# Splitting a pair's TensorE transposes in a pre-norm block's query sweep, and copying the value operands from SBUF

## The chip, the cores and the metric

The kernel runs on one core of one Trainium2 chip. The metric is device microseconds from launch to end; before the change the median of three runs is 2529.96 us (2529.02 to 2530.29).

## The reference

One pre-norm transformer block on 2048 tokens of width 1024, in fp32. The attention goes over the 32 heads *within* each token (32 x 32 scores a token), and the feed-forward weights are rounded to 16 levels (NF4) and scaled back by each block's largest magnitude before use.

```python
def attn(h):                                   # h: 1 x 2048 x 1024
    q = (h @ wq.T + bq).reshape(B, S, H, D)    # H = D = 32
    k = (h @ wk.T + bk).reshape(B, S, H, D)
    v = (h @ wv.T + bv).reshape(B, S, H, D)
    scores = einsum('bshd,bstd->bsht', q, k) / sqrt(D)
    return einsum('bsht,bstd->bshd', softmax(scores), v).reshape(B, S, E)

def ffn(h):
    gate = einsum('bsd,hd->bsh', h, nf4(w1))   # w1, w2: 2752 x 1024
    up   = einsum('bsd,hd->bsh', h, nf4(w2))
    return einsum('bsh,dh->bsd', silu(gate) * up, nf4(w3))

x = x + attn(layernorm(x))
x = x + ffn(layernorm(x))
```

## The kernel before

There are four stages: a sweep for the queries, one for the keys, one for the values with the attention's output, and the feed-forward part. Each sweep goes over eight pairs of 128-token tiles. A pair's projection is a 2 x 2 block product done with seven block products instead of eight (Strassen's scheme in Winograd's form). `products()` does the seven in a fixed order: B11, T3, T2, B21, T1, B22, T4, named by the weight operand. The left operands are seven blocks of the tile `A`: the transposed input blocks `SA11`, `SA12`, `SA22` (and `SA21` in a tile of its own, `a21`), and `S1` to `S4`, the sums and differences that `differences()` forms on VectorE (lines 383 to 386). Each product is eight TensorE matmuls. Products that share a PSUM bank accumulate: bank `z` takes B11, T2, T1; bank `q` takes T3 and T4; in the queries' sweep B22 has its own bank `y`. ScalarE copies a stage of a bank out (line 345), and VectorE adds it to another (lines 362, 366, 374 and 377) to give the two output tiles `ce` and `co`. Line 377 is the last reader of bank `q`; the next pair's T3 writes that bank, which has one buffer.

Between products `products()` calls `fill(n)`, with n running 7, 6, 2, 5, 3, 4. There the sweep places other work in TensorE's order. In the queries' sweep, `fill(5)` (between T1 and B22) holds the next pair's sixteen 128 x 128 transposes (line 458): per tile j two groups of four, each into one PSUM tile `pt` out of three. ScalarE copies each `pt` twice: as it is to `A` (line 461), and with its columns in another order to `V` (line 462), from which the values' sweep's operands are formed by the same `differences()` and stored to DRAM (`opV`, line 473). `A` is stored too (`opD`, line 469), for the keys' sweep. `V` has one buffer: the next pair's copies into it wait until this pair's store of `V` has been read out.

Beside all this runs `background()`, a generator that rounds the feed-forward weights: for each chunk some fifteen VectorE passes over 128 x 1024 numbers (lines 221 to 230), most of them fed by a ScalarE pass into `sg` (line 229), with ScalarE scalings in sixteen pieces before and after (line 182). `advance(n)` emits n of its steps; `flush()` emits the TensorE transposes of a finished chunk (line 156), four at a time. The queries' sweep emits seven steps a pair.

The order of TensorE's instructions is that of the program text. On the other engines and the DMA queue of SyncE a planner orders the instructions at compile time, by the place in the program and by when it expects operands to be ready; on the chip each engine then takes its own list strictly in that order.

Of the kernel before, what the change touches and what calls it, by code (L numbers as in the profile page):

```python
# [14 lines left out]
ALU = mybir.AluOpType  # L15
# [53 lines left out]
def preln_block_kernel(  # L69
# [14 lines left out]
    nc = tc.nc  # L84
# [89 lines left out]
    def flush(steps=3):  # L174
        for _ in range(steps):
            if pending and next(pending[0], flush) is flush:
                pending.pop(0)
# [69 lines left out]
    def advance(n):  # L247
        for _ in range(n):
            next(bg, None)
# [23 lines left out]
    SA11, SA12, SA22, S1, S2, S3, S4 = range(7)  # L273
# [50 lines left out]
    def mm4(dst, w, xop, start, stop):  # L324
        for k in range(4):
# [7 lines left out]
            )  # L333

    def products(A, fill, used=lambda name: None, apart=None):

        def mul(dst, a, w, start, stop):
            mm4(dst, A[:, a], W[w], start, stop)  # L340
            used(w)

        def copied(nm, src):
            t = pair.tile([P, TB], FP, tag=nm, name=nm)
            nc.scalar.copy(t, src)  # L345
            return t

        z = ps_pj.tile([P, TB], FP, tag="z", name="z")
        mul(z, SA11, "B11", True, False)
        g0 = copied("g0", z)  # L350
        q = ps_pj.tile([P, TB], FP, tag="q", name="q")
        mul(q, S3, "T3", True, False)
        s7 = copied("s7", q)
        fill(7)
        mul(z, S2, "T2", False, False)
        u2 = copied("u2", z)
        fill(6)
        r = bank("r")
        mul(r, SA12, "B21", True, True)
        ce = pair.tile([P, E], FP, tag="C0", name="ce")  # L360
        co = pair.tile([P, E], FP, tag="C1", name="co")
        nc.vector.tensor_tensor(ce[:, 0:512], g0, r, ALU.add)
        fill(2)
        mul(z, S1, "T1", False, apart is not None)
        u4 = copied("u4", z)
        nc.vector.tensor_tensor(co[:, 512:], u4, s7, ALU.add)
        fill(5)
        if apart is None:
            mul(z, S4, "B22", False, True)
            nc.scalar.copy(ce[:, 512:], z)  # L370
        else:
            y = apart.tile([P, TB], FP, tag="y", name="y", bufs=1)
            mul(y, S4, "B22", True, True)
            nc.vector.tensor_tensor(ce[:, 512:], u4, y, ALU.add)
        fill(3)
        mul(q, SA22, "T4", False, True)
        nc.vector.tensor_tensor(co[:, 0:512], u2, q, ALU.add)
        fill(4)
        return ce, co

    def differences(t, a21):

        nc.vector.tensor_tensor(t[:, S1], a21, t[:, SA22], ALU.add)
        nc.vector.tensor_tensor(t[:, S2], t[:, S1], t[:, SA11], ALU.subtract)
        nc.vector.tensor_tensor(t[:, S3], t[:, SA11], a21, ALU.subtract)  # L385
        nc.vector.tensor_tensor(t[:, S4], t[:, SA12], t[:, S2], ALU.subtract)

    def qk_T(t, c, b):

        nc.vector.transpose(t, c.rearrange("p (h d) -> p h d", d=D))  # L390
        nc.vector.tensor_tensor(t, t, b.unsqueeze(2).to_broadcast([P, 32, 32]), ALU.add)
# [43 lines left out]
    def load_x(i):  # L435
        xt[i] = work.tile([P, E], FP, tag="x", name="xt", bufs=2)
        nc.sync.dma_start(xt[i], xf[ts(i, P), :])
# [4 lines left out]
    class Inputs:  # L442
# [9 lines left out]
            self.v21 = work.tile([P, 4, P], FP, tag="V21", name="V21")  # L452

        def transposes(self, j):
            for half in range(2):
                pt = ps_t.tile([P, 4, P], FP, tag="pt", name="pt")
                for k in range(4):
                    nc.tensor.transpose(pt[:, k, :], self.xn[j][:, ts(4 * half + k, P)], ident)
                n = (SA11, SA12, SA21, SA22)[2 * j + half]
                a, v = (self.a21, self.v21) if n == SA21 else (self.A[:, n], self.V[:, n])  # L460
                nc.scalar.copy(a, pt)
                nc.scalar.copy(
                    v.rearrange("p k (c m) -> p k c m", c=4),
                    pt.rearrange("p k (m c) -> p k c m", c=4),
                )

        def finished(self):
            differences(self.A, self.a21)
            nc.sync.dma_start(opD[self.p], self.A)

        def finished_v(self):
            differences(self.V, self.v21)
            nc.sync.dma_start(opV[self.p], self.V)
# [12 lines left out]
    nxt = Inputs(0)  # L486
# [9 lines left out]
    def weight_chunk(m, k):  # L496

        b = {}
        for nm in ("B11", "B12", "B21", "B22"):
            b[nm] = work.tile([P, TB], FP, tag=f"c{nm}", name=f"c{nm}")  # L500
            nc.sync.dma_start(b[nm], block(m, int(nm[1]) - 1, int(nm[2]) - 1)[:, k, :])
        t3 = work.tile([P, TB], FP, tag="cT3", name="cT3")
        nc.vector.tensor_tensor(t3, b["B22"], b["B12"], ALU.subtract)
        nc.vector.tensor_tensor(b["B12"], b["B12"], b["B11"], ALU.subtract)
        nc.vector.tensor_tensor(b["B22"], b["B22"], b["B12"], ALU.subtract)
        nc.vector.tensor_tensor(b["B21"], b["B21"], b["B22"], ALU.subtract)
        for n, t in ((1, b["B12"]), (2, b["B22"]), (3, t3), (4, b["B21"])):
            nc.sync.dma_start(wtD[m, n][:, k, :], t)

    def next_W(m):  # L510
        return lambda name: load_W(m, name)

    def load_A(src, p):
        t = pair.tile([P, 7, 4, P], FP, tag="A", name="A", bufs=2)
        nc.sync.dma_start(t, src[p])
        return t

    for p in range(NP):
        more = p + 1 < NP
        now = nxt  # L520
        if more:
            load_x(2 * p + 2)
            load_x(2 * p + 3)
            nxt = Inputs(p + 1)

        def fill(n):
            if n in (7, 3):
                flush(1)
            if n == 5 and more:
                nxt.transposes(0)  # L530
                nxt.transposes(1)
            advance(0 if n == 5 else 1)

        cs = products(now.A, fill, (lambda name: None) if more else next_W("k"), ps_t)
        flush(1)
        if more:
            nxt.finished()
        for j in range(2):
            t = work.tile([P, 32, NH], FP, tag="qd", name="qd", bufs=2)
            qk_T(t, cs[j], qb_sb)  # L540
            nc.sync.dma_start(qD[2 * p + j], t)
        now.finished_v()
        weight_chunk("kv"[p // 4], p % 4)
        advance(2)
        if p == NP - 2:
            first = load_A(opD, 0)
# [63 lines left out]
    for p in range(NP):  # L610
# [12 lines left out]
        for j in range(2):  # L623
            t = work.tile([P, 32, NH], FP, tag="kd", name="kd", bufs=3)
# [74 lines left out]
    for p in range(NP):  # L699
# [32 lines left out]
        for j in range(2):  # L732
            t = work.tile([P, 32, D], FP, tag="vd", name="vd", bufs=3)
# [325 lines left out]
```

## Time and profile before

| | us |
|---|---|
| median of the runs | 2529.96 |
| the profiled execution's own time | 2526.8 |
| span of that execution, first to last instruction | 2525.0 |
| TensorE busy (share of the span) | 2445.7 (97%) |
| VectorE busy | 1923.1 (76%) |
| ScalarE busy | 1564.9 (62%) |
| queries' sweep: start of the first product to start of the keys' first | 13.00 to 244.44 |

TensorE is busy 97% of the span, at a mean granted clock of 0.991. The queries' sweep is the first 10% of the span; in it VectorE is almost as busy as TensorE. A product takes 3.43 us from its start to that of the next one; four 128 x 128 transposes take 0.44 us.

In a timeline's line the first number is the start in us, the second the time the merged instructions took; the bracket at the end is the engine's idle time before them, and what ended it.

### The profile page before, as it was taken

The numbers are of one execution on the slowest core, as the hardware profiler recorded it, in microseconds if no ns is written. First come the engines' busy times: TensorE is split into PE (matmuls) and PEld (weight loads), VectorE is DVE, ScalarE is ACT, GpSimd is POOL, SyncE is SP. The second block draws the span as 40 slices with busy tenths as digits, with TensorE's granted clock in tenths as the row PEclk, the third lists the DMA queues.
The fourth block names the chain that finished last, engine by engine and source line by source line (L and its number), as shares of the span: only waits on it lengthen the run. The fifth ranks groups of instructions, "written<-read, shape, count | busy, mean of one in ns | idle before, by whom it ended". The sixth has DMA issues, their size and how long they took to land.

```text
span 2525.0 us, 36235 instructions
## 1 busy us (share of the span) xinstructions
PE 2445.7 (97%) x14160; PEld 1146.6 (45%) x14160; DVE 1923.1 (76%) x2088; ACT 1564.9 (62%) x3147; POOL 104.9 (4%) x152
## 2 busy tenths in 40 slices
PE   8999999999998999999999999999999999999998
PEld 4444455544444444444444444444444444444433
DVE  8999788878898578978789788887878878851022
ACT  3556544344543478878788787888877888851100
POOL 1010000000000000010000100001000010000100
PEclk9999999999999999999999999999999999999999
DMA  8779633656678574453743547436375353641574
GB/s 306 298 287 358 234 142 129 240 193 214 222 231 298 171 229 113 146 142 134 241 121 136 135 145 238 129 112 159 126 227 151 116 146 126 226 133 63 109 287 141
DMA packets 145323, 464.04 MB, mean 184 GB/s; under 512 B 12352, under 2 KB 66624, under 8 KB 125312
## 3 DMA queue, kind: packets, MB, share of 16 engines
q1 hardware_dynamic: 133056, 419.73, 45.9%
q0 software_dynamic: 11520, 41.95, 9.9%
q8 instruction: 111, 1.82, 0.3%
q14 instruction: 60, 0.49, 0.1%
q10 hardware_dynamic: 576, 0.05, 0.0%
HBM read 275.82 MB, written 185.86 MB: 183 GB/s over the span
## 4 chain that ended last, share of the span: by engine, by line
DVE 29%; PE 25%; ACT 11%; issue 4%; DMA 1%; DVEq 0%; ACTq 0%
DVE r L230 21%; PE po L951 12%; PE z L326 7%; ACT wn L182 4%; ACT r L182 3%; PE q L326 3%; ACT sg L229 2%; DVE r L223 2%; DVE r L225 2%; PE rr L326 1%; DVE am L194 1%; DVE r L241 1%; ACT wop L157 1%; PE po L963 1%; PE ptw L156 0%
## 5 line engine op out<-in xcount | busy, mean ns | idle before, releaser
L229 ACT ACTIVATE sg<-wn 128x1024 f32<-128x1024 f32 x780 | 814.3, 1051 | 358.1 <-DVE r L230 351.5
L230 DVE SCALAR_TENSOR_TENSOR r<-sg,r 128x1024 f32<-128x1024 f32 x780 | 946.9, 1214 | 68.5 <-ACT sg L229 26.2
L951 PE MATMUL po<-w,h 128*128 128x512 f32 x1344 | 594.0, 596 | 6.6 <-ACT acc L975 3.2
L951 PEld LDWEIGHTS po<-w,h 128*128 128x128 f32 x1344 | 250.0, 190 | 324.2 <-issue 288.3
L326 PE MATMUL z<-xB,w 128*128 128x512 f32 x720 | 325.4, 600 | 3.5 <-ACT u L889 1.8
L326 PE MATMUL z<-xT,w 128*128 128x512 f32 x656 | 296.3, 594 | 5.2 <-ACT u L882 5.0
L326 PE MATMUL q<-xT,w 128*128 128x512 f32 x656 | 290.9, 592 | 0.0
L182 ACT ACTIVATE wn<-wn,rc 128x64 f32<-128x64 f32 x1032 | 262.2, 336 | 45.1 <-DVE rc L202 45.1
L326 PEld LDWEIGHTS z<-xB,w 128*128 128x128 f32 x720 | 134.6, 192 | 166.9 <-issue 151.7
L326 PEld LDWEIGHTS q<-xT,w 128*128 128x128 f32 x656 | 123.6, 190 | 151.4 <-issue 149.2
L326 PEld LDWEIGHTS z<-xT,w 128*128 128x128 f32 x656 | 121.9, 190 | 153.9 <-issue 138.2
L326 PE MATMUL q<-wT,A 128*128 128x512 f32 x384 | 174.5, 598 | 2.3 <-DVE A L385 2.3
L326 PE MATMUL z<-wT,A 128*128 128x512 f32 x384 | 175.5, 600 | 1.1 <-ACT u L345 0.8
L326 PE MATMUL z<-wB,A 128*128 128x512 f32 x320 | 152.0, 619 | 13.4 <-ACT u L345 13.4
L182 ACT ACTIVATE r<-r,am 128x64 f32<-128x64 f32 x608 | 153.8, 339 | 14.7 <-DVE r L230 14.7
L326 PE MATMUL rr<-xB,w 128*128 128x512 f32 x328 | 147.5, 592 | 0.0
L975 ACT COPY acc<-po 128x512 f32<-128x512 f32 x160 | 91.3, 571 | 73.0 <-PE po L951 71.3
L194 DVE TENSOR_REDUCE am<-wn 128x16 f32<-128x1024 f32 (+1 forms) x65 | 78.4, 1206 | 76.1 <-ACT r L182 70.0
L981 POOL DMA_DIRECT2D x1d<-acc x80 | 70.2, 877 | 1497.3 <-ACT acc L975 1497.3
L326 PEld LDWEIGHTS q<-wT,A 128*128 128x128 f32 x384 | 72.6, 192 | 90.4 <-issue 84.8
L326 PEld LDWEIGHTS z<-wT,A 128*128 128x128 f32 x384 | 70.3, 190 | 79.8 <-issue 76.7
L885 DVE TENSOR_TENSOR g<-g,rr 128x512 f32<-128x512 f32 x41 | 28.0, 682 | 102.4 <-PE rr L326 102.4
(112 smaller groups left out, 2100.5 us busy)
## 6 DMA issues: line engine op xcount, KB each, us to landing
w<-wd SPq DMA_DIRECT2D x41, 1280.0 KB, 6.9
wd<-wop SPq DMA_DIRECT2D x21, 2048.0 KB, 6.7
x1d<-acc POOLq DMA_DIRECT2D x80, 512.0 KB, 5.1
wn<-in_w_dram SPq DMA_DIRECT2D x63, 512.0 KB, 3.9
w<-wd SPq DMA_DIRECT2D x62, 512.0 KB, 4.1
xT<-xdT SPq DMA_DIRECT2D x28, 1024.0 KB, 7.7
xB<-xdB SPq DMA_DIRECT2D x24, 1024.0 KB, 5.5
opD<-A SPq DMA_DIRECT2D x8, 1792.0 KB, 5.9
```

Source lines behind the costliest of these rows:

```text
L157: nc.scalar.copy(o[:q, first + half], pt[:q])
L182: nc.scalar.mul(dst[:, ts(n, BLOCK)], src[:, ts(n, BLOCK)], by[:, n : n + 1])
L194: nc.vector.tensor_reduce(am[:, :nb], v.rearrange("p (b e) -> p b e", e=BLOCK), AX.X, ALU.max, apply_absolute_value=True,)
L223: nc.vector.scalar_tensor_tensor(r, v, edge, r, ALU.is_lt, ALU.max)
L225: nc.vector.scalar_tensor_tensor(r, v, edge, r, ALU.is_gt, ALU.subtract)
L229: nc.scalar.activation(t, v, AF.Copy, bias=-edge * by, scale=by)
L230: nc.vector.scalar_tensor_tensor(r, t, code, r, ALU.min, ALU.max)
L326: nc.tensor.matmul(dst, w[:, k, :], xop[:, k, :], start=start and k == 0, stop=stop and k == 3, skip_group_check=True,)
L885: nc.vector.tensor_tensor(self.g0, self.g0, r, ALU.add)
L951: nc.tensor.matmul(po, hs[c][j][:, ts(q, P)], w3T[c][:, ts(n, 512)], start=(c == g[0]), stop=(c == g[-1]), skip_group_check=True,)
L975: nc.scalar.copy(a[:, ts(n, 512)], po)
L981: nc.gpsimd.dma_start(x1d[i], a, accum_op=ALU.add)
```

## The change

Three edits, all in the queries' sweep's operands.

1. The next pair's two tiles are no longer transposed together in `fill(5)`. Tile 0 is transposed there (between T1 and B22), tile 1 in `fill(3)` (between B22 and T4).
2. For each tile both copies from PSUM to `A` come first; then both `V` copies, which now read the `A` blocks in SBUF instead of the PSUM tiles. A `pt` tile has one reader in place of two.
3. `differences()` forms S3 before S1 and S2, in the text of the program.

```diff
     def differences(t, a21):
+        nc.vector.tensor_tensor(t[:, S3], t[:, SA11], a21, ALU.subtract)
         nc.vector.tensor_tensor(t[:, S1], a21, t[:, SA22], ALU.add)
         nc.vector.tensor_tensor(t[:, S2], t[:, S1], t[:, SA11], ALU.subtract)
-        nc.vector.tensor_tensor(t[:, S3], t[:, SA11], a21, ALU.subtract)
         nc.vector.tensor_tensor(t[:, S4], t[:, SA12], t[:, S2], ALU.subtract)
...
         def transposes(self, j):
+            copies = []
             for half in range(2):
...
                 nc.scalar.copy(a, pt)
+                copies.append((v, a))
+
+            for v, a in copies:
                 nc.scalar.copy(
                     v.rearrange("p k (c m) -> p k c m", c=4),
-                    pt.rearrange("p k (m c) -> p k c m", c=4),
+                    a.rearrange("p k (m c) -> p k c m", c=4),
                 )
...
         def fill(n):
             if n in (7, 3):
                 flush(1)
-            if n == 5 and more:
-                nxt.transposes(0)
-                nxt.transposes(1)
+            if n in (5, 3) and more:
+                nxt.transposes(0 if n == 5 else 1)
             advance(0 if n == 5 else 1)
```

## Prediction

> **What bounds the kernel now.** I read the page's busy times, then TensorE's waits inside the queries' sweep, then a table of stretches cut at the start of each pair's first product, then the timelines of three engines around one pair. By the page TensorE is the bound, so whatever TensorE loses in the sweep is on the path.
>
> ```profile
> PE 2445.7 (97%) x14160; PEld 1146.6 (45%) x14160; DVE 1923.1 (76%) x2088; ACT 1564.9 (62%) x3147; POOL 104.9 (4%) x152
> ```
>
> TensorE's waits between 26 and 245 us are only these two, both in the transposes that the change moves:
>
> ```profile
> PE pt L458 <- ACT V L462: 12.5, 4, 4.3
> PE pt L458 <- ACT AV L462: 1.0, 3, 0.3
> ```
>
> The stretches of the pairs (us; then busy time and count of TensorE, its weight loads, VectorE, ScalarE, GpSimd; granted clock; DMA share; GB/s), pairs 0 to 7 in order, and at the end the first of the keys' sweep:
>
> ```profile
> 13.00:49.53 36.53, 29.88 (x74) 13.68 (x73) 33.67 (x43) 17.62 (x38) 1.49 (x4) 0.91 0.90 338
> 49.53:82.55 33.02, 28.71 (x74) 13.62 (x72) 29.55 (x44) 15.14 (x33) 3.18 (x6) 0.90 0.67 241
> 82.55:110.31 27.76, 26.44 (x77) 12.71 (x76) 26.93 (x38) 16.97 (x35) 4.29 (x6) 1.00 0.92 332
> 110.31:137.10 26.79, 26.45 (x79) 12.72 (x77) 26.71 (x37) 12.52 (x19) 3.04 (x4) 1.00 0.79 296
> ...
> 190.67:219.53 28.86, 26.00 (x74) 12.32 (x73) 26.82 (x36) 19.86 (x50) 0.00 (x0) 1.00 0.87 340
> 219.53:244.44 24.91, 24.91 (x66) 11.42 (x65) 24.34 (x27) 16.32 (x31) 0.00 (x0) 1.00 0.97 382
> 244.44:275.00 30.56, 28.46 (x68) 12.46 (x67) 29.92 (x31) 26.55 (x67) 0.00 (x0) 1.00 0.86 324
> ```
>
> Pairs 0, 1, 2 and 6 are long, and there VectorE too is almost never idle. That is the second thing to see: TensorE waits for the transposes, yet VectorE has little to spare. Pair 1 in the timelines of TensorE, ScalarE and VectorE:
>
> ```profile
> 66.69 1.47 PE L458 MATMUL pt<-ident,xn 128*128 128x128 f32 x12
> 72.48 1.12 PE L458 MATMUL pt<-ident,xn 128*128 128x128 f32 x4 [4.31 <-ACT V L462]
> 73.39 5.89 PE L326 MATMUL y<-wB,A 128*128 128x512 f32 x8
> 85.98 3.60 PE L326 MATMUL q<-wT,A 128*128 128x512 f32 x8
> ```
>
> ```profile
> 63.84 3.92 ACT L182 ACTIVATE wn<-wn,rc 128x64 f32<-128x64 f32 x16
> ...
> 69.91 0.57 ACT L345 COPY u<-z 128x512 f32<-128x512 f32 x1
> 70.37 1.56 ACT L461 COPY A<-pt 128x512 f32<-128x512 f32 x3
> 71.81 0.62 ACT L462 COPY V<-pt 128x512 f32<-128x512 f32 x1
> ```
>
> ```profile
> 79.31 0.69 DVE L374 TENSOR_TENSOR ce<-u,y 128x512 f32<-128x512 f32 x1 [2.38 <-PE y L326]
> 83.38 0.68 DVE L377 TENSOR_TENSOR co<-u,q 128x512 f32<-128x512 f32 x1
> ```
>
> Three groups of transposes run, and the fourth waits for the first PSUM tile that both copies have left. ScalarE is 3 us late: background scalings stand ahead of `u`, so the copies begin at 70.37 instead of about 67. VectorE has a single hole of any size in the pair, 2.38 us.
>
> **What the edits take off TensorE.** From the first transpose to the start of B22 the seven pairs take 6.42, 6.70, 3.29, 2.31, 2.31, 2.31 and 4.83 us (for pair 1, 73.39 - 66.69), together 28.17. Sixteen transposes at 0.44 us for four (weight transposes, 109.87 to 110.31) are 1.75, seven times 12.25. So 15.9 us are waiting. After the two longest waits the clock is lower: B22 takes 4.62 and 5.72 us to the next product's start in place of 3.43, 3.5 us more. Gross: 19.4 us. In the new order tile 0 needs two of three PSUM tiles and no wait; tile 1 comes 4.3 us later, and its second group needs the tile of the first `A` copy, in pair 1 free at about 70.9 against a need at 71.4. So this wait should go, except a few tenths where ScalarE is late again.
>
> **What VectorE gives back.** Without waits a pair is 7 x 3.43 + 1.75 = 25.8 us on TensorE, plus 0.44 for each weight transposition group. VectorE's work in pairs 1 to 6 is 26.3 to 29.6 us (its column above), so it hardly fits. The coupling is bank `q`: line 377 must have read it before the next T3, which starts one product (3.43 us) after T4 ends. In pair 1 T3 starts at 85.98, line 377 ends at 84.06. So I step through the pairs: the next T3 starts at the later of (this T3 + 25.8 + weight transposes) and the end of line 377. Were VectorE's list unchanged, line 377 could come earlier only by the holes ahead of it: 2.38 us in pair 1, 1.94 in pair 6 (0.39, 0.75, 0.52, 0.28 around its copies), 0.31 in pair 7. The T3s then start at 51.3, 81.7, 110.2, 137.7, 163.9, 191.4, 217.2 and 242.1, against 52.96, 85.98, 113.75, 140.53, 166.88, 194.10, 222.96 and 247.87: 5.8 us saved at the sweep's end. That is the low end. But the background fills what the planner thinks idle, and a shorter pair takes fewer of its passes (1.14 us each). How much shorter the planner sees a pair no row says; the bounds are nothing and the whole wait. I take the wait that pair 2 has with ScalarE in time, 1.32, for pairs 0, 1, 2 and 6 (there the fourth group stands behind four copies), and the 0.34 of pairs 3 to 5 for those. With line 377 earlier by these too, the T3s start at 50.0, 79.0, 106.3, 133.4, 159.3, 186.4, 212.2, 237.1: 10.8 us saved; with 0.56 (2.31 - 1.75) for pairs 3 to 5, 11.4. I take 11. The high end is 19.4, VectorE giving way wherever asked.
>
> **Whether the gain lasts.** Passes pushed out of the sweep, some 6 us, must fit later: in 244 to 275 VectorE is full (29.92 of 30.56), but behind it it has holes of 5.57 us (for a weight load) and 4.03 (for the next pair's B21). They take it; without them the keys' first pairs would wait by as much. ScalarE's 26.55 of 30.56 there is the tighter place: TensorE already waits 2.1 us for a `u` copy, and a reshuffled list could add or save such a wait (its longest elsewhere is 4.3). I put nothing on it, and 4.3 either way in the range.
>
> **Edits and moves costed at nothing.** The `V` copies from SBUF: 32 of them, 0.62 from PSUM now; a 128x1024 SBUF pass is 1.05 and a 128x64 one 0.34, by a straight line 0.67 for 512, so 2 us more in the sweep, on an engine with 7 to 14 us idle a pair; twice that, or 2 us saved, would change the same idle time and no more. S3 first: VectorE's list already has S3 (line 385) first or second in the pairs; in pair 0 it would come 0.6 us earlier, but T2's weights at 24.5 stop TensorE there anyway. Later by 4.3 us are tile 1's copies, the S blocks, the `opD` store on SyncE's queue (behind it the `qD`, `opV` and weight stores; SyncE waits 42.1 us in the sweep for the last S block already, and the stores are read in later sweeps), and the second `xn` tile's release: VectorE's next normalisation into it must now stand behind tile 1's transposes, and behind it the pair's sums. It is needed a pair later, 20 us, and costs only if the list has it early.
>
> ScalarE's list is in order, and a `V` copy waits for the last store of `V` (5.8 us median to landing). The trace shows no ScalarE wait for a DMA in the sweep; if one `V` copy came 2 us early in each pair, the copies and `u` behind it would be late by that, against 4.6 us of spare time below. [...]
>
> On the clock: waits of 4.04 and 4.31 us were followed by a slow B22, one of 2.86 by a full-speed one (3.43). My stepping leaves one wait of 3.25 us, ahead of pair 2's T3, between these rows; it costs nothing, or 1.2 to 2.3 us as before. I take nothing. [...]
>
> **Rivals.** *TensorE's whole wait returns* (chance 0.2): the planner thins the background and VectorE keeps up as in pairs 3 to 5; 14 to 19.4 us, centre 2513. For it: those pairs run 2 us behind without stopping TensorE. Against: pairs 0 and 1, where VectorE is full because of the start. *Forecast, half returns* (0.45): 6 to 14 us. *VectorE's list is as before, or the keys' sweep takes the gain back* (0.2): 0 to 5.8 us, centre 2525. *The diff does less than it says* is in here: if the fourth group still waits for late copies. *Slower* (0.15): S3 is late. Tile 1's first transpose to the next T3 is 0.87 + 3.43 + 3.43 = 7.7 us; in pair 3 S3 starts 3.1 us after the last group now. Spare: 4.6 us; from a lag above that the next pair's T3 waits. ScalarE's lag was 3 us in pair 1, VectorE's 2 to 4. If each of seven T3s waited a product's time, 24.0 us would go against 19.4 saved: 2535. This decides only if the two lags add up in every pair.
>
> **How the numbers follow.** The profiled execution's 2526.8 (span 2525.0 and 1.8 around it) would be 2515.8; the median of the runs is 3.2 above it, so 2529.96 - 11 = 2519. Range: 19.4 off and some of the 4.3 either way gives 2509; the upper end, 2531, takes in the no-gain case and a little of the slower one. About 0.2% (5 us) is what a measurement can tell from no change: the first two cases (0.65) are faster, the third is within but for 0.01 that is faster, and of the last 0.13 is slower and 0.02 within: 0.66, 0.21, 0.13.
>
> **What would show it.** Right: the wait of transposes for ScalarE copies below 2 us in the sweep, B22 at 3.43 in pairs 0 and 1, T3's wait for line 377 appearing in pairs 0 to 2, the keys' first product at about 233.5, the rest shifted by the same. Wrong: T3 waiting for line 385; the keys' sweep starting early and the values' at the old time; the transposes still waiting.

## The result and the profile after

The change makes the kernel slower: 2542.06 us (median of 4 runs, 2539.05 to 2545.86) against 2530.12 (2529.02 to 2530.54), a ratio of 1.0049 with a 95% interval of 1.0031 to 1.0066. The forecast was 2519.0 with a range up to 2531; both its sign and its range missed. The profiled execution took 2539.05 us with a span of 2537.3, 12.3 more than before's 2525.0.

The busy times of the page of after, first. TensorE's work is the same (2445.7 before), so some 11 of the 12 us are idle time; ScalarE has 17.4 us more.

```profile
PE 2447.2 (96%) x14160; PEld 1146.9 (45%) x14160; DVE 1923.7 (76%) x2088; ACT 1582.3 (62%) x3147; POOL 100.2 (4%) x152
```

TensorE's waits in after (waited for: us in total, times, longest), the first three between 13 and 236 us, the last two between 236 and 300. Before had 12.5 + 1.0 us on ScalarE's `V` copies in the first stretch. They are gone; the new rows are one wait for an `A` copy (2.6), one for a normalised tile `xn` (5.2) and one for line 377 (1.6). In the second stretch before had only a `u` wait of 2.1. After has a wait of 13.4 us for a DMA, the load of the query tiles `ql` for the first attention scores.

```profile
PE pt L459 <- DVE xn L321: 5.2, 1, 5.2
PE pt L459 <- ACT A L462: 2.6, 1, 2.6
...
PE q L326 <- DVE co L377: 1.6, 1, 1.6
...
PE sc L406 <- DMA ql<-qD: 13.4, 1, 13.4
PE z L326 <- ACT u L345: 3.8, 1, 3.8
```

TensorE's timeline of after, at the places that matter:

```profile
72.38 3.68 PE L326 MATMUL q<-wT,A 128*128 128x512 f32 x8
...
121.75 1.97 PE L459 MATMUL pt<-ident,xn 128*128 128x128 f32 x8 [5.22 <-DVE xn L321]
123.51 5.01 PE L326 MATMUL y<-wB,A 128*128 128x512 f32 x8
...
258.84 5.40 PE L326 MATMUL z<-wB,A 128*128 128x512 f32 x8 [3.82 <-ACT u L345]
264.08 3.60 PE L326 MATMUL q<-wT,A 128*128 128x512 f32 x8
...
270.94 3.60 PE L326 MATMUL q<-wT,A 128*128 128x512 f32 x8
287.98 1.77 PE L406 MATMUL sc<-kd,ql 32*32 32x32 f32 x128 [13.44 <-DMA ql<-qD]
289.68 5.63 PE L326 MATMUL z<-wT,A 128*128 128x512 f32 x8
```

The same place before:

```profile
274.28 3.60 PE L326 MATMUL q<-wT,A 128*128 128x512 f32 x8
277.80 1.79 PE L406 MATMUL sc<-kd,ql 32*32 32x32 f32 x128
279.52 3.70 PE L326 MATMUL z<-wT,A 128*128 128x512 f32 x8
```

The T3 at 72.38 stood at 85.98 before: TensorE is 13.6 us ahead. At the keys' first T3 it is still 6.74 ahead (241.13 against 247.87), at the second pair's T3 3.34 ahead (270.94 against 274.28). One block product after that come the first scores, and at the second pair's T4 it is 12.09 **behind** (309.71 against 297.62). From there on the difference stays between 11.4 and 16.3 us, and it is 12.3 at the end. So what turns the lead into the loss arises at one place, between 274 and 295 us: 13.44 us of wait, and 1.94 us because the product behind it takes 5.47 us to the next one's start instead of 3.53.

Why `ql` is late is read from SyncE's list of DMA issues, after first, then before:

```profile
245.34 0.36 SPq L477 DMA_DIRECT2D opV<-AV  x1
245.74 2.82 SPq L505 DMA_DIRECT2D cB<-in_wvT_dram  x4
...
272.30 0.33 SPq L512 DMA_DIRECT2D wtDv<-cB  x1
...
277.27 1.63 SPq L608 DMA_DIRECT2D ql<-qD  x3
```

```profile
207.54 5.13 SPq L501 DMA_DIRECT2D cB<-in_wvT_dram  x4
...
258.47 1.04 SPq L605 DMA_DIRECT2D ql<-qD  x2
```

The sweep's last `weight_chunk` loads four weight blocks (`cB`), subtracts on VectorE, and stores the results (`wtDv`). Before, its loads are issued at 207.5. After, they stand behind the last store of `V`, at 245.7, its subtractions come only at 270 to 276, and its stores, which SyncE must issue ahead of the `ql` loads, hold SyncE for 20 us:

```profile
SPq L512 <- DVE cB L508: 20.3, 1, 20.3
```

No other transfer is issued in that time, and those under way end before it does: the DMA engines' busy tenths of after between 235 and 300 us (40 slices of 1.6 us) have a gap of six slices, from 262.6 to 272.4. It is not bandwidth that `ql` lacks:

```profile
DMA  9999999999998999800000059798999992000000
```

VectorE in after, just ahead of the scores. The chunk's subtractions (lines 507 to 510) stand between background passes, and all four steps that make the keys' tiles `kd` stand behind them, though `co`, their last input, was done at 268.4:

```profile
269.85 0.68 DVE L507 TENSOR_TENSOR cT<-cB,cB 128x512 f32<-128x512 f32 x1
...
275.06 0.69 DVE L510 TENSOR_TENSOR cB<-cB,cB 128x512 f32<-128x512 f32 x1
275.66 1.22 DVE L230 SCALAR_TENSOR_TENSOR r<-sg,r 128x1024 f32<-128x1024 f32 x1
276.80 1.24 DVE L390 STREAM_TRANSPOSE kd<-ce 128x1024 f32<-128x1024 f32 x1
...
279.08 2.32 DVE L391 TENSOR_TENSOR kd<-kd,kb 128x1024 f32<-128x1024 f32 x2
```

Before, the first transposition of `kd` began at 268.96 and the last step ended at 275.45, 3.5 us after `co` (271.23 to 271.91); in after it ends at 281.4, 13 us after `co`.

### The profile page after: what moved, and what is told of

The parts are those of the page before. It is cut to its first block, busy times and chain, and to the rows that moved or that the text cites. A ratio compares the mean times of both kernels' runs of the same rounds, so it can differ in the third digit from the quotient of the medians.

```text
span 2537.3 us, 36232 instructions
## 1 busy us (share of the span) xinstructions
PE 2447.2 (96%) x14160; PEld 1146.9 (45%) x14160; DVE 1923.7 (76%) x2088; ACT 1582.3 (62%) x3147; POOL 100.2 (4%) x152
## 4 chain that ended last, share of the span: by engine, by line
DVE 29%; PE 25%; ACT 10%; issue 4%; DMA 0%; DVEq 0%; ACTq 0%
DVE r L230 21%; PE po L954 12%; PE z L326 7%; ACT wn L182 4%; ACT r L182 3%; PE q L326 3%; ACT sg L229 2%; DVE r L223 2%; DVE r L225 2%; PE rr L326 1%; DVE am L194 1%; DVE r L241 1%; ACT wop L157 1%; PE po L966 1%; PE ptw L156 0%
```

## The experiments

Four theories. **Q**: SyncE's list, held by the late last chunk, makes the loss. **B**: the `V` copies from SBUF are dear on ScalarE, and that costs part of the sweep's gain. **C**: VectorE too is late with `kd`, so a freed SyncE gives only part back. **V**: the sweep has no room, and what is pushed out of it lands ahead of the first scores in any order. Positions are microseconds against before, each in its profiled execution; minus is ahead. A ratio is taken against runs of before in the same session (medians of before 2527.75 to 2530.12), so two medians of the table can't be compared to the last microsecond. Positions vary as well: ql_pool's lists of TensorE, VectorE and ScalarE are the change's up to the first scores, and it stands 1.07 us behind it at the keys' first T3. The profiled execution of copies_only took 6 us more than that kernel's median, that of psumv_pool 3 us more, that of before 3 us less.

| kernel | median us | ratio to before (95%) | keys' first T3 | 2nd pair's T3 | 2nd pair's T4 |
|---|---|---|---|---|---|
| the change | 2542.06 | 1.0049 (1.0031-1.0066) | -6.74 | -3.34 | +12.09 |
| s3_only | 2533.65 | 1.0024 (1.0014-1.0033) | +0.67 | +0.78 | +7.00 |
| split_only | 2535.43 | 1.0025 (1.0016-1.0035) | -1.53 | -2.33 | +6.35 |
| copies_only | 2531.62 | 1.0017 (1.0007-1.0027) | -3.17 | -3.73 | +5.19 |
| chunk_pool | 2532.76 | 1.0009 (0.9998-1.0019) | -6.73 | -7.07 | +1.33 |
| before_pool | 2530.70 | 1.0009 (0.9999-1.0018) | +0.31 | +0.31 | +0.32 |
| ql_pool | 2535.75 | 1.0024 (1.0014-1.0033) | -5.67 | -2.27 | +6.25 |
| after_early | 2541.17 | 1.0052 (1.0037-1.0067) | -3.21 | +2.61 | +14.06 |
| before_early | 2533.25 | 1.0021 (1.0012-1.0031) | +3.50 | +3.10 | +3.09 |
| split_early | 2532.90 | 1.0020 (1.0010-1.0031) | -1.84 | -2.60 | +4.39 |
| psumv_early | 2528.21 | 1.0004 (0.9992-1.0015) | +0.42 | -0.74 | -0.71 |
| psumv_pool | 2524.65 | 0.9988 (0.9976-1.0000) | -1.41 | -2.58 | -2.61 |
| vpool | 2545.58 | 1.0066 (1.0051-1.0081) | +8.23 | +8.91 | +17.17 |

### The edits one by one

**s3_only**: the kernel before, with S3 formed first and nothing else.

```diff
+        nc.vector.tensor_tensor(t[:, S3], t[:, SA11], a21, ALU.subtract)
         nc.vector.tensor_tensor(t[:, S1], a21, t[:, SA22], ALU.add)
         nc.vector.tensor_tensor(t[:, S2], t[:, S1], t[:, SA11], ALU.subtract)
-        nc.vector.tensor_tensor(t[:, S3], t[:, SA11], a21, ALU.subtract)
```

> The kernel before with S3 formed first and nothing else. In the changed kernel the keys' sweep's first scores wait 13.4 us for the load of the queries (ql), which stands in SyncE's list behind the stores of the last weight chunk; those wait 20.3 us for VectorE, since the last chunk's loads were put behind the last store of V. Theory Q (SyncE's list): that placement is the planner's answer to any small shift of the text; here too the planned list has the last chunk's four loads behind the last store of V, so the scores should wait 8 to 14 us for ql though the transposes are as before: 2535 to 2545, slower than before by 0.2 to 0.6%. Theory B (the V copies from SBUF make ScalarE and VectorE late): nothing of it is in here, so 2528 to 2532, no wait for ql. Theory C (VectorE's backlog catches a faster sweep): the sweep is not faster, so 2528 to 2532.

The edit that I took as free costs 0.24%. The wait that theory Q named is there, at about half its size; the time lies between Q's range and that of B and C. The edit leaves the transposes' waits where they were (11.7 us of 12.5) and the sweep's end within 0.7 us, but the last chunk's four loads move from 207.5 to 252.05, the `ql` loads to 274.01, and TensorE waits for them:

```profile
PE sc L406 <- DMA ql<-qD: 4.6, 1, 4.6
```

**split_only**: the transposes in two places, the copies and S3 as before.

```diff
-            if n == 5 and more:
-                nxt.transposes(0)
-                nxt.transposes(1)
+            if n in (5, 3) and more:
+                nxt.transposes(0 if n == 5 else 1)
```

> Only the transposes' split; the V copies read PSUM as before and S3 is third. The planned list has three of the last chunk's four loads ahead of the keys' weights and the fourth behind the last store of V, so the chunk is as late as in the changed kernel. Theory Q: the sweep ends 5 to 12 us earlier, the scores then wait for ql by 8 to 14 us: 2526 to 2540. Theory B: V copies at 0.6 us, ScalarE not later than before: the sweep's gain stays, 2515 to 2522. Theory C: the gain is lost without a single long wait, 2525 to 2532.

The split alone takes only 2.6 us off the transposes' waits for `V` (13.5 to 7.8 + 3.1), since each PSUM tile still waits for two copies. The wait for `ql` is 6.9 us, under Q's 8 to 14, and the sweep gains 1.5 us, not 5 to 12; the time lies in Q's range. B and C missed.

**copies_only**: the copies of the change, both tiles still transposed in `fill(5)`.

```diff
                 nc.scalar.copy(a, pt)
-                nc.scalar.copy(v..., pt...)
+                copies.append((v, a))
+            for v, a in copies:
+                nc.scalar.copy(v..., a...)
```

> Only the order and source of the copies (both A copies of a tile first, then V copies from SBUF); all sixteen transposes in one place, S3 third. V copies take 1.16 us instead of 0.62, 17 us more of ScalarE in the sweep. Theory Q: planned list again has the last chunk's loads behind the last store of V: first scores wait 8 to 14 us for ql; the transposes' wait for V copies (13.5 us) becomes a smaller wait for A copies: 2528 to 2542. Theory B: ScalarE's and VectorE's lag costs by itself: TensorE waits for u copies or VectorE in the sweep rise by 10 us or more, 2535 to 2545 with no wait for ql. Theory C: 2525 to 2532.

The wait for `V` becomes a wait for `A` copies of 11.1 us in six places; the wait for `ql` is 7.8 us. The time, 2531.62 us, lies in the ranges of Q and of C; the wait for `ql` is one that only Q has. B missed. Edit 2 and edit 1 each do little alone; together they take the wait away. All three single edits, in different parts of the sweep, end with the last chunk late (in split_only one of its four loads, behind the last store of `V`, in the others all). So I infer that the planner's order of SyncE's list is sensitive to small shifts, whatever the edit is for; its reasoning is in no profile. Not every edit does it: in before_pool (below) the last chunk's loads stay at 206.3.

### SyncE's list and VectorE's

**chunk_pool**: the change, with the chunks' stores issued by GpSimd. **before_pool** is the control: the same edit in the kernel before.

```diff
-            nc.sync.dma_start(wtD[m, n][:, k, :], t)
+            nc.gpsimd.dma_start(wtD[m, n][:, k, :], t)
```

> The changed kernel with the weight chunks' stores issued from GpSimd's queue instead of SyncE's, so that nothing behind them on SyncE waits for the chunks. Theory Q: the wait of the first scores for ql falls from 13.4 to under 4 us, and the sweep's gain of 6 to 8 us stays: 2515 to 2526, faster than before. Theory B: VectorE and ScalarE are as loaded as in the changed kernel, so a wait of similar length comes back elsewhere: 2535 to 2545. Theory C: 2528 to 2540.

> Control for the run with the chunks' stores on GpSimd's queue: the kernel before with that one edit and nothing of the change. Theory Q: the kernel before has its last chunk early, so its stores hold nothing up on SyncE; moving them is worth nothing, within 3 us of before (2525 to 2533). Rival: the move is a gain of its own, 5 us or more in any kernel, and then the 9 us that it gave the change say nothing of the change.

In the change the edit gives 10.8 us at the second pair's T4 (+12.09 to +1.33), and about 10 us of time (0.40%), to 2532.76, which lies in C's range alone; in the kernel before it gives nothing (+0.32). The wait for `ql` is gone, `ql` being issued at 264.39. TensorE now waits at the same instruction for VectorE:

```profile
PE sc L406 <- DVE kd L391: 6.3, 1, 6.3
```

This wait and the slow product behind it (5.48 instead of 3.53) make 8.3 us, and they alone turn a lead of 7.07 us into a lag of 1.33.

**ql_pool**: the sharper test of Q against C. Only the first two `ql` loads move; TensorE's and VectorE's lists are exactly those of the change.

```diff
-            nc.sync.dma_start(t, src[2 * p + j])
+            (nc.gpsimd if tag == "ql" and p == 0 else nc.sync).dma_start(t, src[2 * p + j])
```

> The change as it is, except that the two loads of the first pair's query tiles (ql, line 608, pair 0 of the keys' sweep) are issued by GpSimd, whose list holds no wait for the last weight chunk there, instead of SyncE. The lists of TensorE and VectorE are those of the change. Theory Q (SyncE's list alone makes the wait of 13.4 us): the wait is gone whole and the scores start some 13 us earlier, near 274.5 us; with the slow clock behind the wait (about 2 us) the time falls by 13 to 15 us, to about 2527. Theory C (VectorE is late as well, since the last chunk's subtractions stand ahead of the keys' transposition): the wait for ql is replaced by a wait for the keys' tile kd; in the change VectorE ends kd at about 281.4 us against a start of the scores at 287.98, so only 6 to 7 us come back, and the time is about 2535.

TensorE's timeline of ql_pool at the scores:

```profile
281.39 1.80 PE L406 MATMUL sc<-kd,ql 32*32 32x32 f32 x128 [5.79 <-DVE kd L391]
283.47 6.00 PE L326 MATMUL z<-wT,A 128*128 128x512 f32 x8 [0.28 <-ACT g L345]
```

2535.75 us, where C gave about 2535 and Q 2527. SyncE's list cost 5.8 us (+12.09 to +6.25); the rest of the loss is `kd`, late in VectorE's list. The two stand in parallel: taking away one shows the other. The late last chunk has a part in both: its stores stand ahead of `ql` on SyncE, its subtractions ahead of `kd` on VectorE. On VectorE it is the smaller part: of the 8.4 us from the end of `co` (268.4) to the first step of `kd` (276.8) in after, the four subtractions take 2.4 and five background passes 5.7. In s3_only the subtractions come late as well (268.75 to 273.11), and `kd` ends at 277.64, only 2.2 us later than before.

**after_early**: the change, with `weight_chunk` called ahead of a pair's products instead of behind them, so that the last chunk comes earlier. **before_early** is its control.

```diff
+        weight_chunk("kv"[p // 4], p % 4)
         ...
         cs = products(now.A, fill, ...)
         ...
-        weight_chunk("kv"[p // 4], p % 4)
```

> The changed kernel with each pair's weight chunk emitted ahead of the pair's products instead of behind them, which gives its loads, sums and stores an earlier place in the planned lists (in SyncE's list the last chunk's stores now stand ahead of the last store of V and of every ql). Theory Q (the last chunk came a stage too late; it held SyncE's list and, on VectorE, stood ahead of the keys' first kd tile): no wait of the scores for ql, and under 2 us for kd; the keys' first T3 at about 241 and the second pair's B21 product at about 276 to 278: 2515 to 2524. Theory V (VectorE's room: what is pushed out of the sweep comes between the sweep and the first scores, whatever the chunk does): a wait of 4 to 8 us for kd stays, 2526 to 2534.

> The kernel before with the weight chunks emitted early, as a control. Its last chunk was in time, so by theory Q nothing is to be had but small shifts: 2522 to 2532, no wait for ql or kd, the transposes' wait for V copies still 8 to 14 us. By theory V the same.

Theory Q alone fails here. The wait for `ql` is gone and that for `kd` is 1.1 us, yet nothing is won. TensorE's two longest waits of after_early between 236 and 300 us:

```profile
PE z L326 <- ACT g L345: 7.2, 1, 7.2
PE q L326 <- DMA wT<-wtDk: 3.8, 1, 3.8
```

The keys' weight loads now stand behind the chunk's stores on SyncE, and the `g` copy behind background passes on ScalarE which themselves wait for VectorE. The control costs 3 us too, in the sweep (its waits for `V` copies grow to 13.5 + 3.5), so some of it belongs to the early call itself. Theory V's forecast fails too: it had a wait of 4 to 8 us for `kd` and 2526 to 2534 us. What is left of V is its general idea, and that is argued and not shown: moving the chunk gave no order in which none of the three lists is late. The control, forecast at 2522 to 2532, came out just above.

**split_early**: split_only, with the chunk called early.

> Only the split, with early chunks; V copies from PSUM directly behind each A copy, S3 third. Split alone left waits of 10.9 us for V copies, since a V copy that waits for the store of V holds its PSUM tile. Theory Q: no wait for ql, the rest as in the split alone: 2522 to 2530. Theory V: 2528 to 2536.

No wait for `ql`, but `g` late by 4.8 us at the same place (+4.39), the same replacement in a milder form; 2532.90 us is in V's range and above Q's.

### The copies

**psumv_early** and **psumv_pool**: the change, but with the `V` copies read from PSUM (both `A` copies still first); the chunk called early in the one, the chunks' stores on GpSimd in the other.

```diff
-                copies.append((v, a))
-            for v, a in copies:
-                nc.scalar.copy(v..., a...)
+                copies.append((v, pt))
+            for v, pt in copies:
+                nc.scalar.copy(v..., pt...)
```

> The changed kernel with early chunks, and the V copies again read the PSUM tiles (after both A copies of the tile), 0.6 us each instead of 1.16: 17 us less of ScalarE in the sweep. If ScalarE's load cost anything in the sweep (TensorE waited 2.6 us for an A copy that stood behind three V copies), TensorE waits for transposes' buffers less than 3 us in the sweep still, since in the split a tile's two PSUM tiles have a product's time to come free; the sweep ends 2 to 6 us earlier than with the SBUF copies: 2511 to 2522. If the source does not matter: the same as with SBUF copies within 3 us. Theory V: 2526 to 2534.

> The change with both A copies first, but the V copies read from PSUM as before, and the chunks' stores on GpSimd's queue. Theory B (the V copies from SBUF cost ScalarE 17 us and with it part of the sweep's gain) together with Theory Q: the transposes' wait for V copies comes back in part (5 to 11 us of the 13.5), ScalarE's busy time falls by 17 us, and the time lies between 2524 and 2530. Rival (Theory C: the sweep is bound by VectorE at its end, whatever ScalarE does): the keys' sweep starts no earlier than in the kernel before, and the time is that of before or above, 2528 to 2535.

With the PSUM reads the waits for `V` copies come back in the sweep (11.2 + 2.9 us in the one, 6.8 + 3.8 in the other), and the sweep ends where before's does or 1.4 us earlier. But ScalarE is 17 us less busy, and neither `ql` nor `kd` is late. Between kernels whose text differs in nothing but the copies' source, the step from the second pair's T3 to its T4 is -0.03 against +8.40 (psumv_pool and chunk_pool), and +0.03 against +11.45 (psumv_early and after_early, where the chunk is early in both). So in both pairs the loss behind the sweep goes with the copies' source. It is not the only way to it: s3_only and split_only read PSUM and lose there too. Theory B as stated fails: it had the SBUF copies spoil the sweep's gain, and with them the sweep ends earlier. The forecast of psumv_early, 2511 to 2522 us and under 3 us of waits for transposes' buffers, missed by 6 us and by 11; that of psumv_pool came true. How much of the loss is the 17 us themselves and how much the order that the planner finds with them is not separated (the lists of VectorE, ScalarE and SyncE differ in many places): in psumv_pool it places the last chunk's loads at 209.8, in chunk_pool the subtractions come at 264.6 to 269.9. psumv_pool is the best of these kernels, 0.9988 of before with an interval that touches 1. The change with PSUM reads and nothing else was not run.

**vpool**: the change with the `V` copies on GpSimd, and the chunks' stores there too.

```diff
-                nc.scalar.copy(v..., a...)
+                nc.gpsimd.tensor_copy(v..., a...)
```

> The change with the V copies on GpSimd instead of ScalarE (still from the A copies in SBUF), and the chunks' stores on GpSimd's queue. Theory B: ScalarE loses 37 us of copies in the sweep (32 of 1.16 us), no A copy stands behind a V copy, and the sweep keeps more of its 13 us: the keys' sweep starts 9 to 13 us earlier than before and the time is 2515 to 2525. Rival: GpSimd takes over 2 us for a copy and slows VectorE beside it, or its norm operations (line 118) come later behind the copies and the x tiles with them: the keys' sweep starts no earlier than in the change (237.7), and the time is 2530 or above.

The slowest of all. A copy takes 1.54 us, and VectorE's passes beside one are stretched: while three copies run from 80.28 to 85.14, a subtraction takes 1.59 us instead of 0.69 and a background pass 2.13 instead of 1.22.

```profile
80.50 1.59 DVE L509 TENSOR_TENSOR cB<-cB,cB 128x512 f32<-128x512 f32 x1
82.02 2.13 DVE L230 SCALAR_TENSOR_TENSOR r<-sg,r 128x1024 f32<-128x1024 f32 x1
```

VectorE is 18 us busier in all (1941.3), the first scores wait 6.7 us for `kd`, and T3 waits for line 377, the coupling through bank `q` that the prediction stepped through. The rival of the expectation came true here, though a copy took less than its 2 us:

```profile
PE q L326 <- DVE co L377: 10.5, 5, 4.2
```

## Why the prediction was wrong

**What the edits take off TensorE** was right, but for one wait of 2.6 us for an `A` copy where the prediction allowed a few tenths. The waits for `V` copies went from 13.5 us to none, B22 of pair 1 is at 3.44 (61.20 to the transposes at 64.64) instead of 5.72, and T3 behind it came 13.6 us earlier.

**What VectorE gives back** was mis-sized in both directions. The forecast T3s of pairs 1 and 2 were 50.0 and 79.0; they came at 46.60 and 72.38, so VectorE gave way more than I let it. The later ones, forecast 133.4 and 237.1, came at 136.10 and 241.13. The pair that starts with the T3 at 101.49 took 34.61 us instead of before's 26.78. This is a cost that I named and dropped: "the second `xn` tile's release ... costs only if the list has it early". It was not the release: SyncE and VectorE waited for none there. The tiles of `x` are loaded at 110.32 (before: two at 89.11), now behind a store of `V` that waited for the last S block until 95.40, one of `A` until 101.98, and a chunk's four stores, which wait for subtractions on VectorE:

```profile
109.09 1.18 SPq L512 DMA_DIRECT2D wtDk<-cB  x1
110.32 1.60 SPq L437 DMA_DIRECT2D xt<-in_x_dram  x2
```

The loads land 5.8 to 6.0 us after their issue, and VectorE, without a hole from 99.5 to 120.5, comes to the tile at 117.41; so the load and VectorE's own list are late together, and which alone would have held the tile is not shown. With `xn` done at 121.7, the transposes wait 5.22 us and B22 runs at a lower clock (0.54 in the 5 us from 121.75). Line 377 was waited for once, 1.6 us, and not in pairs 0 to 2. The sum at the keys' first T3 was 6.74 against the 11 forecast. chunk_pool has no wait for `xn` in the sweep, but ends it at -6.73 as well, with new waits for ScalarE in its place (2.3 and 2.3); so the 5.2 are not to be had by that alone.

**Whether the gain lasts** is the step that failed. I sized the place where the chain turns into the keys' sweep by VectorE's free time (holes of 5.57 and 4.03 us) and a longest `u` wait of 4.3, and put "nothing on it, and 4.3 either way in the range". It cost 18.8: 3.4 for a `u` copy that is 1.7 us later (3.82 against 2.10, and the slow product behind it), and 15.4 at the first scores. The holes were the wrong measure. VectorE is busy 25.62 of the 30 us from 245 to 275, less than before (29.36), and had run 59 of the background's line-230 passes by 274 us, against 60. It was not overfull; its order had changed, and so had SyncE's: of the 15.4 us, 5.8 went with SyncE's list (ql_pool), and the wait that then stood there was VectorE's `kd`.

**Edits and moves costed at nothing** failed in two items. S3 first: the working looked at VectorE's order in each pair, where it is indeed worth nothing, but not at what any shift does to the lists that the planner writes (s3_only: 0.24%). The stores: "the stores are read in later sweeps" asks when their data is needed. What mattered is who stands behind them in SyncE's list: behind the last chunk's four stores stood `ql`, needed at 274 us. The prediction named the weight stores as queued behind `opD`, and did not ask what was queued behind them. The trace of before had the rows, SyncE's waits between 13 and 245 us at these stores, of which the two largest are:

```profile
SPq L508 <- DVE cB L505: 10.1, 7, 1.9
SPq L508 <- DVE cB L504: 6.1, 7, 2.0
```

The third item, the `V` copies, was off by its size. A straight line through two other passes gave 0.67 us; it measured 1.14 in the groups of the first 250 us (after first, then before; busy us, mean ns):

```profile
L466 ACT COPY AV<-A 128x512 f32<-128x512 f32 x24 | 25.9, 1141 | 1.2 <-DMA opV<-AV 1.2
```

```profile
L462 ACT COPY AV<-pt 128x512 f32<-128x512 f32 x24 | 14.2, 625 | 0.0
```

That is 17 us, not 2. I wrote that twice the extra "would change the same idle time and no more"; against that, psumv_early and after_early differ in the text by the copies' source only, and their ratios are 1.0004 and 1.0052 (psumv_pool and chunk_pool: 0.9988 and 1.0009, with intervals that just meet). ScalarE's idle time, given as 7 to 14 us a pair, is 7.6 to 18.9 by the trace of before. The copy reads every fourth fp32 number, 16 bytes apart. From PSUM that step cost next to nothing: 0.61 us without it (line 461 of before, the copies to `A`), 0.62 with it. Why the stepped copy takes 1.8 times as long from SBUF is not shown; the same copy from SBUF without the step was not run. The straight line came from contiguous passes. The worry about ScalarE waiting for the `V` store was rightly put low: 1.2 us in the whole sweep.

**The rivals.** The slower case had S3 late in every pair; T3 waited for S3 (line 385 before, 383 in after) only at the start, 1.7 us against 2.3 before. That the kernel got slower, as this case said, is luck: it came by another mechanism. The third case had the right place, "the keys' sweep takes the gain back", but bounded the damage at no gain; the keys' sweep took the gain and 12 us more. (Its centre, from 0 to 5.8 us off 2529.96, is 2527 and not 2525.) Of the listed signs, "the keys' sweep starting early and the values' at the old time" came nearest: the keys' sweep started early and everything behind its first pair came 12 us late.

What stays open: why the planner places the last chunk late in the change and in each of its three edits alone, and how much of the change's loss S3 bears within it (the change without S3 was not run).

## What to carry to other kernels

Cost a moved step also by its place in each in-order list: for every store or load of that stretch ask what is issued behind it, and when that is needed. Where a planner writes the lists, an edit that is free by itself can reorder them, so look first at the places where one stage hands over to the next, and at the loads needed soonest there. A price for a copy must come from a row with the same source and stride: here a line through other rows gave 0.67 us, and the copy took 1.14.

## What the runs showed of the hardware

- VectorE, ScalarE, GpSimd and SyncE took their lists in order: by source line, VectorE's 2088 instructions, ScalarE's 3157, GpSimd's 152 and SyncE's 592 issues stand in the traces of before and of after in the order of the planner's lists (ScalarE has two table loads besides).
- SyncE's list, taken in order, left the DMA engines idle: six slices of nothing in after, from 262.6 to 272.4, while `ql` was ready to be loaded (in ql_pool GpSimd issued its loads at 259.5). Issuing these two loads from GpSimd saved 5.8 us (ql_pool): SyncE's list was held by a wait of 20.3 us, and the issue of each of the four stores took 0.32 to 0.42 us.
- A strided ScalarE copy of 128 x 512 fp32 from SBUF took 1.14 us (after), and 0.62 from PSUM with the same stride (before).
- Beside three GpSimd copies from SBUF (vpool, 80.28 to 85.14) two subtractions on VectorE took 1.59 and 1.61 us instead of 0.69, and a background pass 2.13 instead of 1.22.
- The length of a wait alone did not tell whether TensorE's clock drops behind it. By the timelines' durations, in before the T3 behind a wait of 2.30 us took 5.40 us, at a granted clock of 0.68, and the B22 behind one of 2.86, with four transposes between, took 3.60 at 1.00. After 1.77 (chunk_pool, before B22 at 256.81) and 2.58 (after, the transposes at 93.69) the next product took 3.70 and 3.60 us, after 3.82 (after) it took 5.40, at 0.67. So the two rows of before that the prediction went by, full speed after 2.86 us and slow after 4.04, do not bound a threshold. Lines of before:

```profile
18.97 5.40 PE L326 MATMUL q<-wT,A 128*128 128x512 f32 x8 [2.30 <-DVE A L385]
...
212.17 0.66 PE L458 MATMUL pt<-ident,xn 128*128 128x128 f32 x4 [2.86 <-ACT V L462]
212.66 3.60 PE L326 MATMUL y<-wB,A 128*128 128x512 f32 x8
```
